# Two adjacency columns per transposed element, and eight-step cycles in the first pass of a graph attention kernel

## The chip, the cores and the metric

The kernel runs on one core of one Trainium2 chip. Times are device microseconds of one launch, from the first to the last instruction, as the hardware profiler takes them. A core has TensorE (PE in the profile; its weight loads are listed apart as PEld), VectorE (DVE), ScalarE (ACT), GpSimd (POOL) and SyncE (SP). POOL and SP are used here mostly to issue DMAs: POOL for those on the software queue, among them every DMA that changes the type of its data, SP for the others. Before the change the kernel took 2134.29 us, the median of 3 runs (2130.82 to 2136.55).

## What is computed

There are 4096 nodes with 512 features and a 0/1 adjacency of 4096 x 4096 in fp32, which is symmetric and has ones on its diagonal. Layer 0 is a graph attention layer with 8 heads of 64 features, layer 1 an attention within 32 graphs of 128 nodes. Each layer is followed by a residual sum and a normalisation. Layer 0, the part that matters here:

```python
feats = einsum('nf,hfo->hno', X, W)
dense = s_self[:, :, None] + s_neigh[:, None, :]     # per head, 4096 x 4096
dense = where(dense > 0, dense, 0.2 * dense)
attn = softmax(dense * A[None], axis=-1)
out = einsum('hij,hjo->hio', attn, feats) + b
```

The score of an edge is a sum of one number of node i and one of node j, so its exponential is a product, and the leaky slope makes it the larger of two products. The kernel uses this: per head and neighbour j it forms `q = max(p_i, d_j) * A[j, i]` and lets TensorE sum `q` against scaled features. No 4096 x 4096 exponential is ever taken.

## The kernel before, in words

The nodes are cut into 32 tiles of 128 neighbours j (a step works on one of them) and 4 chunks of 1024 nodes i. The order is fixed by hand on PE (its instructions keep the order of the program); the other engines' instructions are placed by a scheduler that moves them among each other.

**Setup** (to about 165 us). Eight blocks of four tiles. For block k, PE transposes the rows of x (`turn_rows`, L631), computes the features of four tiles (`features`, L699, four fp32 matmuls of 512 columns each), the two scores per head (`scores` L640 for the block after, and `exponentials` L654), and turns the exponentials of the self scores, p and u, from columns into rows (`rows_of_exponentials`, L689). ACT copies those rows to SBUF (`pu_row`, L693), from where a DMA writes them to DRAM. ACT and DVE make scaled features out of each tile (`scaled_features`, L706 to L730: `gst`, and `fst` on ACT L717 and DVE L718), and POOL writes them to DRAM as g_d and f_d. There are two buffers each for `fst` and `gst`, so the third `fst` of a block waits until the write of the first has landed. After blocks 4 and 5 POOL issues the first two adjacency loads (L758, L573).

**Four passes over the adjacency**, two heads each (`main_pass`). A pass runs over the 4 chunks, a chunk over its 32 steps in cycles of `wide` steps: 4 in passes 0 and 3, 8 in passes 1 and 2. In a cycle:

- DVE makes `q` for each step and each of the two heads (L1285); ACT makes a 0/1 `mark` of each (L1294), and DVE makes every eighth mark (L1290);
- PE sums the raw adjacency against the features into `accf` (L1305), then `q` against scaled features into `acc` (L1321), and every eight steps the marks into `dens` (L1335); in pass 0 also the row sums `ae` (L1346 to L1354, in the profile at L1348);
- the adjacency tiles `at` of the next cycle are brought, `wide - 2` of them after `accf` and the others at the cycle's end (`follow`, L1312 and L1355).

**Bringing a tile** (`bring`, L1051). In passes 1 to 3 it is a DMA from at_d. In pass 0 the adjacency comes from the input, where it has nodes i on rows, and is needed with j on partitions: POOL loads 1024 x 512 values and turns them into bf16 on the way (`a_bf`, L571 to L575, two buffers), PE transposes the eight 128 x 128 blocks of a step into PSUM (L1063), ACT casts them to fp32 (L1064), and POOL writes the tile to at_d for the later passes (L1065). `at` and `q` have six buffers each; passes 1 and 2 add six and two more (`ring`, `more`).

At the end of a chunk DVE takes the sums out of PSUM (`ys`), and small pieces of work (transposes L1128, L1147, L1170) are put among the matmuls of the next chunk. Layer 1 follows the last pass and is woven into its end.

Of the kernel before, what the change touches and what calls it, by code (L numbers as in the profile page):

```python
# [10 lines left out]
F32 = mybir.dt.float32  # L11
BF16 = mybir.dt.bfloat16
I32 = mybir.dt.int32
AF = mybir.ActivationFunctionType
# [5 lines left out]
P = 128  # L20
ALPHA = 0.2
# [374 lines left out]
F32R = mybir.dt.float32r  # L396
# [8 lines left out]
def adjacency_streamed_path(  # L405
# [29 lines left out]
    nc = tc.nc  # L435
    N, F = x.shape
    H, _, FH = W.shape
    NT = N // P
    FC = F // P
# [116 lines left out]
    def ring(name, pool, n):  # L556

        if name not in more:
            return pool
        k = turns[name] % (n + more[name][1])  # L560
        turns[name] += 1
        return pool if k < n else more[name][0]
# [1 line left out]
    ats = {}  # L564
    a_bs = {}
    pools = {}
    pools["adj"] = first_pass.enter_context(tc.tile_pool(name="adjp", bufs=2, side="right"))

    def load_adjacency(c, j):

        a_b = pools["adj"].tile([P, CT, 4 * P], BF16, name="a_bf")  # L571
        a_bs[c, j] = a_b
        return nc.gpsimd.dma_start(  # L573
            a_b, adj[ts(c, C), j * P : (j + 4) * P].rearrange("(t p) n -> p t n", p=P)
        )  # L575


    with tc.tile_pool(name="setup1", bufs=1, side="right") as one, tc.tile_pool(
# [2 lines left out]
        name="xtp", bufs=4, side="right"  # L581
    ) as xtp, tc.tile_pool(name="ps_setup", bufs=7, space=PSUM) as pss:
        NB = NT // 4
        xts, xTs, sts = {}, {}, {}

        def load_rows(k):
            xts[k] = []
# [62 lines left out]
        def exponentials(k):  # L650
            blk = slice(4 * k, 4 * k + 4)
            pts = pss.tile([P, 4, 2, H], F32, name="ps_set")
            for u in range(4):
                nc.tensor.matmul(  # L654
                    pts[:, u].rearrange("p k h -> p (k h)"),
                    sts[k][:, ts(u, P)],
                    stack,
                    start=(u == 0),
                    stop=True,
                    skip_group_check=True,  # L660
                )
            s_c, t_c = pts[:, :, 0, :], pts[:, :, 1, :]
            nc.scalar.activation(e_all[:, blk, 1, :], t_c, AF.Exp)
            nc.scalar.activation(e_all[:, blk, 0, :], t_c, AF.Exp, scale=ALPHA)
            nc.scalar.activation(d_all[:, blk, :], t_c, AF.Exp, scale=ALPHA - 1.0)
            nc.scalar.activation(u_all[:, blk, :], s_c, AF.Exp, scale=-ALPHA)
            nc.scalar.activation(p_all[:, blk, :], s_c, AF.Exp, scale=1.0 - ALPHA)


            nc.vector.tensor_scalar_mul(  # L670
                nb_all[:, blk, :], d_all[:, blk, :], -BIG * (1.0 + 2.0**-23)
            )
            eb = e_b[:, blk]
            for i in range(2):
                src = e_all[:, blk, i, :]
                rest = small.tile([P, 4, H], F32, name="rest")
                nc.vector.tensor_copy(eb[:, :, :, 3 * i], src)
                nc.vector.tensor_sub(rest, src, eb[:, :, :, 3 * i])
                nc.vector.tensor_copy(eb[:, :, :, 3 * i + 1], rest)
                nc.vector.tensor_sub(eb[:, :, :, 3 * i + 2], rest, eb[:, :, :, 3 * i + 1])  # L680
            nc.vector.tensor_copy(
                e_p[:, blk, :NE].rearrange("p j (m h) -> p j h m", h=H), eb[:, :, :, :3]
            )
            nc.vector.tensor_scalar_mul(eb[:, :, :, :3], eb[:, :, :, :3], -1.0)

        def rows_of_exponentials(k):
            pr = pss.tile([2 * H, 4, P], F32, name="ps_set")
            for u in range(4):
                nc.tensor.transpose(  # L689
                    pr[:, u, :], pu_all[:, 4 * k + u].rearrange("p k h -> p (k h)"), ident  # L690
                )
            row = one.tile([2 * H, 4 * P], F32, name="pu_row")
            nc.scalar.copy(row, pr.rearrange("p u n -> p (u n)"))  # L693
            nc.gpsimd.dma_start(pu_d[:, ts(k, 4 * P)], row)

        def features(k, u):
            pf = pss.tile([P, H * FH], F32, name="ps_set")
            for c in range(FC):
                nc.tensor.matmul(  # L699
                    pf, xTs[k][:, c, u, :], w_sb[:, c, :], start=(c == 0), stop=(c == FC - 1)  # L700
                )
            fb = three.tile([P, H, FH], F32, name="fb")
            nc.vector.tensor_add(fb.rearrange("p h o -> p (h o)"), pf, b_row)
            return fb
# [28 lines left out]
        for k in range(NB):  # L733
            if k + 1 < NB:
                load_rows(k + 1)
            fbs = [features(k, 0)]
            if k == 0:
                fbs.append(features(k, 1))
                scores(0)
            else:  # L740
                exponentials(k)
            if k + 1 < NB:
                turn_rows(k + 1)
            if k == 0:
                exponentials(0)
            scaled_features(k, 0, fbs[0])
            if k:
                fbs.append(features(k, 1))
            scaled_features(k, 1, fbs[1])
            fbs.append(features(k, 2))  # L750
            scaled_features(k, 2, fbs[2])
            if k + 1 < NB:
                scores(k + 1)
            rows_of_exponentials(k)
            fbs.append(features(k, 3))
            scaled_features(k, 3, fbs[3])
            if k in (4, 5):
                tc.keep_in_program_order(load_adjacency(0, 4 * (k - 4)))  # L758
        xsum = one.tile([P, FC], F32, name="xsum")
        nc.vector.tensor_reduce(xsum, xs, AX.X, OP.add)  # L760
# [289 lines left out]

    def bring(r, c, j):  # L1051

        at = ring("at", atp, 6).tile([P, C], F32R, name="at")
        ats[r, c, j] = at
        if r:
            nc.sync.dma_start(at.bitcast(F32), at_d[c, j])
            return
        if j % 4 == 0 and (c, j) not in a_bs:
            load_adjacency(c, j)
        a_b = a_bs[c, j - j % 4]  # L1060
        pt = misc([P, CT, P], BF16)
        for t in range(CT):
            nc.tensor.transpose(pt[:, t, :], a_b[:, t, ts(j % 4, P)], ident_b)  # L1063
        nc.scalar.copy(at, pt.rearrange("p t n -> p (t n)"))  # L1064
        nc.gpsimd.dma_start(at_d[c, j], at.bitcast(F32))  # L1065

    def load_block():

# [169 lines left out]
    def main_pass(r, ae=None, wide=4):  # L1238

        for c in range(NCH):  # L1240
# [19 lines left out]
            for j0 in range(0, NT, wide):  # L1260
# [41 lines left out]
                for j in cycle:  # L1302
                    for w in range(2):
                        for s in range(2):
# [4 lines left out]
                                start=(j == 0 and w == 0),  # L1309
                                stop=(j == NT - 1 and w == 1),  # L1310
                            )
                for x_ in follow[: wide - 2]:  # L1312
                    bring(*x_)
                if r:
                    pieces(c, j0 // 4, 0)
# [26 lines left out]
                if r == 0:  # L1342
                    for j in cycle:

                        a_j = ats[r, c, j].bitcast(BF16).rearrange("p (n k) -> p n k", k=2)
                        for s in range(2):  # L1346
# [5 lines left out]
                                start=(j < 2),  # L1352
                                stop=(j >= NT - 2),
                            )  # L1354
                for x_ in follow[wide - 2 :]:  # L1355
                    bring(*x_)
                first = (at_step - NT * NCH) // 4
                for group in range(first, first + wide // 4) if r else ():
                    if group == 0:
                        load_block()  # L1360
                        load_block()
                    for _ in range(1 + (group % 3 == 2)):
                        check_block(done[0])
                        done[0] += 1
                        load_block()
            ends.append(sums_to_rows(r, c, acc, accf, ae, u_row, 0.75 * wide))

    done = [0]
    with tc.tile_pool(name="ps_ae", bufs=1, space=PSUM) as psx, tc.tile_pool(
        name="aes", bufs=1  # L1370
    ) as pools["aes"]:
        ae = psx.tile([P, HB], F32, name="ae")
        nc.vector.memset(ae, 0.0)
        banks.append(psx)
        main_pass(0, ae)
        run_pieces(999.0)
        banks.remove(psx)
    first_pass.close()
    banks.extend([ctx.enter_context(tc.tile_pool(name="ps_misc2", bufs=2, space=PSUM))] * 2)
    with tc.tile_pool(name="keep_f", bufs=1) as keep:  # L1380
        with tc.tile_pool(name="more_at", bufs=MORE) as at2, tc.tile_pool(
            name="more_q", bufs=2
        ) as q2:
            more["at"], more["q"] = (at2, MORE), (q2, 2)
            for x_ in steps[NT * NCH : NT * NCH + 8]:
                bring(*x_)
            with tc.tile_pool(name="wl1", bufs=1, side="right") as wp:
                work.append(weights_of_layer_1(keep, wp))
                work.append(kind_of_graphs(wp))
                kind_of_scores(wp)  # L1390
                main_pass(1, wide=8)
                for gen in work:
                    for _ in gen:
                        pass
                work.clear()
            main_pass(2, wide=8)
            more.clear()
        with tc.tile_pool(name="lp", bufs=2) as lp, tc.tile_pool(
            name="lp1", bufs=1
        ) as lp1, tc.tile_pool(name="lp2", bufs=2) as lp2:  # L1400
            pools.update(lp=lp, lp1=lp1, lp2=lp2)
            main_pass(3)
            plan["K"] = kind_of_inputs(lp1)
            run_plan("bEpppaaRaaKKbbababaababbbb")


@with_exitstack
# [50 lines left out]
```

## Time and profile before

| | busy us | share of the span |
|---|---|---|
| PE | 2091.5 | 98% |
| DVE | 1660.8 | 78% |
| ACT | 1537.5 | 72% |
| POOL | 249.5 | 12% |
| span of the profiled run | 2136.1 | |
| adjacency loads on POOL (L573), 32 | 12.7 us to landing | |
| writes of `at` (L1065), 128 | 11.8 us to landing | |

A line of a group reads: line, engine, operation, what is written from what, shape, count, then busy us and mean ns of one, then the idle time of the engine just before and what ended it. A line of the timeline reads: start in us, length in us, engine, line, operation, names and shape, how often in a row; a bracket gives idle time before it and what ended it. A matmul's length in the profile contains its latency, and neighbours overlap; where it matters, the difference of starts is what PE spends. The lines of the DMA queues are packets, MB, and the time that the packets took as a share of 16 engines' span.

### The profile page before, as it was taken

To read this page: it belongs to the slowest core of one execution; us is meant where nothing else is said; L and a number is where in the kernel's file an instruction comes from. 1 tells how busy PE (TensorE), PEld (TensorE's weight loads), DVE (VectorE), ACT (ScalarE), POOL (GpSimd) and SP (SyncE) were. 2 spreads that over 40 slices of the span, in tenths; PEclk is the share of its full clock that TensorE was granted. 3 is DMA by queue.
4 is the path that set the end of the run, shared out by engine and by line. 5 is a ranking of instruction groups with operands and counts; after the bars stand their busy time and mean duration, and the time that the engine had idled before them with its cause. 6 is when DMAs were issued, how large, how long until landed. Compare 5 with 4: busy or idle time off the path is not lost. (4 is left out here: it accounts for less than half of the span.)

```text
span 2136.1 us, 39020 instructions
## 1 busy us (share of the span) xinstructions
PE 2091.5 (98%) x15492; PEld 1036.8 (49%) x15492; DVE 1660.8 (78%) x2024; ACT 1537.5 (72%) x1820; POOL 249.5 (12%) x391
## 2 busy tenths in 40 slices
PE   8999999999999999999999999999999999999987
PEld 4545455555555444544454454444444444445443
DVE  5557777778688878799999999999974884886554
ACT  3337777878777988789998989999876566567420
POOL 2332222222210000000000000000310210110110
PEclk9999999999999999999999999999999999999999
DMA  8889999999999998789999999989964774674211
GB/s 249 277 236 293 321 294 287 300 272 307 270 296 320 337 320 273 259 291 348 332 325 334 312 338 332 331 290 357 320 227 150 239 246 144 218 270 163 70 47 42
DMA packets 207885, 568.13 MB, mean 266 GB/s; under 512 B 25292, under 2 KB 66252, under 8 KB 207692
## 3 DMA queue, kind: packets, MB, share of 16 engines
q1 hardware_dynamic: 140748, 425.79, 58.0%
q0 software_dynamic: 62784, 138.69, 23.5%
q8 instruction: 124, 2.03, 0.4%
q10 hardware_dynamic: 4160, 1.05, 0.2%
q14 instruction: 69, 0.57, 0.1%
HBM read 491.79 MB, written 107.22 MB: 280 GB/s over the span
## 5 line engine op out<-in xcount | busy, mean ns | idle before, releaser
L1285 DVE SCALAR_TENSOR_TENSOR q<-p_row,d_all,at 128x1024 f32<-128x1024 f32 x1024 | 1244.6, 1279 | 213.2 <-PE acc L1321 138.7
L1294 ACT ACTIVATE mark<-q,nb_all 128x1024 fp8e4<-128x1024 f32 x896 | 995.3, 1143 | 242.4 <-DVE q L1285 220.6
L1321 PE MATMUL acc<-q,g_s 128*32 128x512 f32 x8192 | 906.7, 593 | 3.0 <-DVE q L1285 2.5
L1321 PEld LDWEIGHTS acc<-q,g_s 128*32 128x32 f32 x8192 | 260.6, 110 | 591.5 <-issue 528.4
L1305 PE MATMUL accf<-at,f_s 128*128 128x512 f32 x2048 | 499.2, 398 | 2.0 <-DMA f_s<-f_d 1.7
L1305 PEld LDWEIGHTS accf<-at,f_s 128*128 128x128 f32 x2048 | 377.1, 189 | 113.2 <-issue 29.3
L1079 ACT ACTIVATE ck<-ck,neg_half_f 128x1024 f32<-128x1024 f32 x128 | 145.9, 1140 | 21.9 <-DMA ck<-in_adj_dram 21.7
L1080 ACT ACTIVATE ck<-ck,neg_quarter 128x1024 f32<-128x1024 f32 x128 | 146.3, 1143 | 1.8
L1064 ACT CAST at<-ps_m 128x1024 fp32r<-128x1024 bf16 x128 | 122.7, 1010 | 6.3 <-PE ps_m L1063 4.5
L1335 PE MATMUL dens<-mark,e_b 128*6 128x512 fp8e4 x2048 | 125.1, 381 | 0.0
L1006 PE MATMUL ps_m<-wvT,x1T 128*128 128x512 f32 x256 | 114.3, 594 | 4.1 <-DVE parts L1150 4.0
L934 PE MATMUL ps_m<-x1T,M_sb 128*128 128x512 f32 x256 | 115.9, 607 | 1.8 <-ACT x1T L915 1.8
L699 PE MATMUL ps_set<-w_sb_f,xT_f 128*128 128x512 f32 x256 | 114.5, 600 | 0.0
L1183 POOL DMA_DIRECT2D hs_d<-hst x12 | 10.7, 895 | 838.3 <-DVE hst L1171 736.1
L1290 DVE TENSOR_SCALAR mark<-q,d_all 128x1024 fp8e4<-128x1024 f32 x128 | 95.8, 748 | 3.2
L1335 PEld LDWEIGHTS <-e_b 128*6 128x6 bf16 x2048 | 53.4, 86 | 83.1 <-issue 40.1
L1065 POOL DMA_DIRECT2D at_d<-at x128 | 68.6, 536 | 172.9 <-ACT at L1064 171.0
L717 ACT ACTIVATE fst<-fb 128x512 fp32r<-128x512 f32 x32 | 20.3, 634 | 93.6 <-DMA f_d<-fst 65.6
L934 PEld LDWEIGHTS ps_m<-x1T,M_sb 128*128 128x128 f32 x256 | 49.0, 194 | 65.4 <-issue 62.5
L1006 PEld LDWEIGHTS ps_m<-wvT,x1T 128*128 128x128 f32 x256 | 47.7, 190 | 60.1 <-issue 57.4
L699 PEld LDWEIGHTS ps_set<-w_sb_f,xT_f 128*128 128x128 f32 x256 | 48.3, 194 | 54.2 <-issue 53.8
L1014 DVE TENSOR_TENSOR v_t<-ps_m,bv_row 128x512 f32<-128x512 f32 x32 | 21.8, 681 | 63.5 <-PE ps_m L1006 63.5
(169 smaller groups left out, 1204.9 us busy)
## 6 DMA issues: line engine op xcount, KB each, us to landing
at<-at_d SPq DMA_DIRECT2D x384, 512.0 KB, 5.8
ck<-in_adj_dram SPq DMA_DIRECT2D x128, 512.0 KB, 5.4
f_s<-f_d SPq DMA_DIRECT2D x128, 512.0 KB, 7.7
at_d<-at POOLq DMA_DIRECT2D x128, 512.0 KB, 11.8
g_s<-g_d SPq DMA_DIRECT2D x128, 256.0 KB, 5.8
a_bf<-in_adj_dram POOLq DMA_DIRECT2D x32, 1024.0 KB, 12.7
f_d<-fst POOLq DMA_DIRECT2D x32, 512.0 KB, 6.4
p_row<-pu_d SPq DMA_DIRECT2D x32, 512.0 KB, 6.9
```

Source lines behind the costliest of these rows:

```text
L699: nc.tensor.matmul(pf, xTs[k][:, c, u, :], w_sb[:, c, :], start=(c == 0), stop=(c == FC - 1))
L934: nc.tensor.matmul(pz, L1["M"][:, f, ts(c, P)], x1T[:, f, :], start=(f == 0), stop=(f == FC - 1),)
L1006: nc.tensor.matmul(pv, x1T[:, f, ts(u, P)], L1["wvT"][:, f, :], start=(f == 0), stop=(f == FC - 1),)
L1064: nc.scalar.copy(at, pt.rearrange("p t n -> p (t n)"))
L1079: tc.keep_in_program_order(nc.scalar.activation(ck, ck, AF.Square, bias=neg_half))
L1080: nc.scalar.activation(ck, ck, AF.Abs, bias=neg_quarter, accum_out=binp[:, k : k + 1])
L1285: nc.vector.scalar_tensor_tensor(q, p_row[h], d_j, ats[r, c, j].bitcast(F32), op0=OP.max, op1=OP.mult)
L1290: nc.vector.tensor_scalar(mark, q, d_j, None, op0=OP.is_gt, saturate=False)
L1294: nc.scalar.activation(mark, q, AF.Sigmoid, bias=nb_all[:, j, hh : hh + 1], scale=BIG, saturate=False,)
L1305: nc.tensor.matmul(accf[:, s, :], f_s[j // 4][:, j % 4, w, :], ats[r, c, j][:, ts(s, HB)], start=(j == 0 and w == 0), stop=(j == NT - 1 an ...
L1321: nc.tensor.matmul(acc[o : o + 32, s, :], g_s[j // 4][:, j % 4, h, o % FH : o % FH + 32], qs[j, h][:, ts(s, HB)], start=(j == 0), stop=(j ...
L1335: nc.tensor.matmul(dens[lo : lo + 6, :], e_b[:, j, 2 * r + h, :], marks[j, h][:, ts(s, HB)], start=(j == 0), stop=(j == NT - 1),)
```

## The change

The adjacency holds only zeros and ones, which an 8-bit float holds exactly. The load in pass 0 now makes 8-bit floats, and two neighbouring columns of a row are taken together as one 16-bit element. A transpose moves 16-bit elements unchanged, so one transpose now turns 256 columns instead of 128, and the number of transposes halves. What lands on a partition is a pair: an even and an odd node. ACT casts the even bytes into one `at` tile and the odd bytes into another. So a tile of neighbours is no longer 128 nodes in a row, but the even or the odd ones among 256.

Everything that belongs to a neighbour has to follow that order: features and exponentials are computed for the even and odd nodes by weights with a step of two (`tile_j`). What belongs to a node i keeps the plain order: the row copy puts p and u back into it, and a new function, `columns_of_exponentials`, turns these rows into columns again for the chunk ends.

The loads get a third buffer and a third early issue after block 6. Pass 0 now has cycles of eight steps like passes 1 and 2, with their rings of 12 and 8 buffers; four tiles are brought after `accf` and four at the cycle's end. The pools of those rings are opened before pass 0. The aim is to take transposes and the switches between short cycles off PE in the first pass.

```diff
-    pools["adj"] = first_pass.enter_context(tc.tile_pool(name="adjp", bufs=2, side="right"))
+    pools["adj"] = first_pass.enter_context(tc.tile_pool(name="adjp", bufs=3, side="right"))
...
 
-        a_b = pools["adj"].tile([P, CT, 4 * P], BF16, name="a_bf")
+        a_b = pools["adj"].tile([P, CT, 4 * P], FP8, name="a_b8")
...
-        xts, xTs, sts = {}, {}, {}
+        xts, xTs, sts, pu_js, rows = {}, {}, {}, {}, {}
+
+        def tile_j(x, u):
+
+            return x.rearrange("p (q n k) -> p q n k", q=2, k=2)[:, u // 2, :, u % 2]
...
-                    sts[k][:, ts(u, P)],
+                    tile_j(sts[k], u),
...
-            nc.scalar.activation(u_all[:, blk, :], s_c, AF.Exp, scale=-ALPHA)
-            nc.scalar.activation(p_all[:, blk, :], s_c, AF.Exp, scale=1.0 - ALPHA)
+            pu_j = pu_js[k] = two.tile([P, 4, 2, H], F32, name="pu_j")
+            nc.scalar.activation(pu_j[:, :, 1, :], s_c, AF.Exp, scale=-ALPHA)
+            nc.scalar.activation(pu_j[:, :, 0, :], s_c, AF.Exp, scale=1.0 - ALPHA)
...
-            row = one.tile([2 * H, 4 * P], F32, name="pu_row")
-            nc.scalar.copy(row, pr.rearrange("p u n -> p (u n)"))
+                    pr[:, u, :], pu_js[k][:, u].rearrange("p k h -> p (k h)"), ident
+                )
+            row = rows[k] = one.tile([2 * H, 4 * P], F32, name="pu_row")
+            nc.scalar.copy(
+                row.rearrange("p (q n k) -> p q k n", q=2, k=2),
+                pr.rearrange("p (q k) n -> p q k n", q=2),
+            )
             nc.gpsimd.dma_start(pu_d[:, ts(k, 4 * P)], row)
+
+        def columns_of_exponentials(k):
+            pc = pss.tile([P, 4, 2 * H], F32, name="ps_set")
+            for u in range(4):
+                nc.tensor.transpose(pc[:, u, :], rows[k][:, ts(u, P)], ident[: 2 * H, : 2 * H])
+            nc.vector.tensor_copy(
+                pu_all[:, 4 * k : 4 * k + 4].rearrange("p u k h -> p u (k h)"), pc
+            )
 
...
                 nc.tensor.matmul(
-                    pf, xTs[k][:, c, u, :], w_sb[:, c, :], start=(c == 0), stop=(c == FC - 1)
+                    pf,
+                    tile_j(xTs[k][:, c].rearrange("p u n -> p (u n)"), u),
+                    w_sb[:, c, :],
+                    start=(c == 0),
+                    stop=(c == FC - 1),
                 )
...
             rows_of_exponentials(k)
             fbs.append(features(k, 3))
             scaled_features(k, 3, fbs[3])
-            if k in (4, 5):
+            columns_of_exponentials(k)
+            if k in (4, 5, 6):
                 tc.keep_in_program_order(load_adjacency(0, 4 * (k - 4)))
...
     def bring(r, c, j):
 
-        at = ring("at", atp, 6).tile([P, C], F32R, name="at")
-        ats[r, c, j] = at
         if r:
+            at = ats[r, c, j] = ring("at", atp, 6).tile([P, C], F32R, name="at")
             nc.sync.dma_start(at.bitcast(F32), at_d[c, j])
+            return
+        if j % 2:
             return
         if j % 4 == 0 and (c, j) not in a_bs:
             load_adjacency(c, j)
-        a_b = a_bs[c, j - j % 4]
+        pairs = a_bs[c, j - j % 4].rearrange("p t n -> p (t n)").bitcast(BF16)
+        pairs = pairs.rearrange("p (t k n) -> p t k n", t=CT, k=2)[:, :, j % 4 // 2, :]
         pt = misc([P, CT, P], BF16)
         for t in range(CT):
-            nc.tensor.transpose(pt[:, t, :], a_b[:, t, ts(j % 4, P)], ident_b)
-        nc.scalar.copy(at, pt.rearrange("p t n -> p (t n)"))
-        nc.gpsimd.dma_start(at_d[c, j], at.bitcast(F32))
+            nc.tensor.transpose(pt[:, t, :], pairs[:, t, :], ident_b)
+        both = pt.rearrange("p t n -> p (t n)").bitcast(FP8).rearrange("p (n k) -> p n k", k=2)
+        for k in range(2):
+            at = ats[r, c, j + k] = ring("at", atp, 6).tile([P, C], F32R, name="at")
+            nc.scalar.copy(at, both[:, :, k])
+            nc.gpsimd.dma_start(at_d[c, j + k], at.bitcast(F32))
...
-                for x_ in follow[: wide - 2]:
+                first = wide // 2 if r == 0 or wide == 4 else 6
+                for x_ in follow[:first]:
                     bring(*x_)
...
-                for x_ in follow[wide - 2 :]:
+                for x_ in follow[first:]:
                     bring(*x_)
...
     done = [0]
+    keep = ctx.enter_context(tc.tile_pool(name="keep_f", bufs=1))
+    wide_passes = ExitStack()
+    at2 = wide_passes.enter_context(tc.tile_pool(name="more_at", bufs=MORE))
+    q2 = wide_passes.enter_context(tc.tile_pool(name="more_q", bufs=2))
+    more["at"], more["q"] = (at2, MORE), (q2, 2)
...
-        main_pass(0, ae)
+        main_pass(0, ae, wide=8)
...
-    with tc.tile_pool(name="keep_f", bufs=1) as keep:
-        with tc.tile_pool(name="more_at", bufs=MORE) as at2, tc.tile_pool(
-            name="more_q", bufs=2
-        ) as q2:
-            more["at"], more["q"] = (at2, MORE), (q2, 2)
-            for x_ in steps[NT * NCH : NT * NCH + 8]:
-                bring(*x_)
...
+    more.clear()
+    wide_passes.close()
```

## The prediction

> **What bounds the kernel now.** I read the page first: what is busy, and who waits.
>
> ```profile
> PE 2091.5 (98%) x15492; PEld 1036.8 (49%) x15492; DVE 1660.8 (78%) x2024; ACT 1537.5 (72%) x1820; POOL 249.5 (12%) x391
> ```
>
> TensorE (PE) is busy 98% of the span and its groups show almost no idle time, so a stage ends when its matmuls end, and what a change takes off PE's stream is worth its full length while the feeders keep up. Second, the groups kept apart by shape, for what the change halves:
>
> ```profile
> L1064 ACT CAST at<-ps_m 128x1024 fp32r<-128x1024 bf16 x128 | 122.7, 1010 | 6.3 <-PE ps_m L1063 4.5 <-issue 1.1 <-ACT mark L1294 0.7
> L1063 PE MATMUL ps_m<-ident_b,a_bf 128*128 128x128 bf16 x1024 | 69.0, 221 | 1.3 <-ACT at L1064 1.3
> ```
>
> 1024 transposes cost 69 us of PE, all in the first pass (165 to 632 us). Third, PE's timeline over eight steps of that pass, for the spacing of the starts:
>
> ```profile
> 384.34 0.63 PE L1348 MATMUL ae<-at,e_p 128*25 128x512 bf16 x8
> 384.90 1.07 PE L1063 MATMUL ps_m<-ident_b,a_bf 128*128 128x128 bf16 x16
> 385.78 3.92 PE L1305 MATMUL accf<-at,f_s 128*128 128x512 f32 x16
> 389.54 1.07 PE L1063 MATMUL ps_m<-ident_b,a_bf 128*128 128x128 bf16 x16
> 390.54 7.07 PE L1321 MATMUL acc<-q,g_s 128*32 128x512 f32 x64
> 397.43 1.91 PE L1335 MATMUL dens<-mark,e_b 128*6 128x512 fp8e4 x32
> 399.15 0.63 PE L1348 MATMUL ae<-at,e_p 128*25 128x512 bf16 x8
> 399.72 1.07 PE L1063 MATMUL ps_m<-ident_b,a_bf 128*128 128x128 bf16 x16
> 400.59 3.96 PE L1305 MATMUL accf<-at,f_s 128*128 128x512 f32 x16
> 404.40 1.07 PE L1063 MATMUL ps_m<-ident_b,a_bf 128*128 128x128 bf16 x16
> ```
>
> No bracket with a wait: the matmuls follow one another. Fourth, the DMA queues between 200 and 600 us, because this is the pass that both loads and writes the adjacency:
>
> ```profile
> q0 software_dynamic: 44954, 87.43, 83.8%
> q1 hardware_dynamic: 10135, 29.40, 21.2%
> ```
>
> Last, the setup, where the change adds a wait. ScalarE (ACT) and PE around block 5:
>
> ```profile
> 118.64 0.63 ACT L717 ACTIVATE fst<-fb 128x512 fp32r<-128x512 f32 x1 [2.58 <-DVE fb L703]
> 129.89 0.63 ACT L717 ACTIVATE fst<-fb 128x512 fp32r<-128x512 f32 x1 [10.62 <-DMA f_d<-fst]
> 130.43 0.57 ACT L648 COPY st<-ps_set 128x512 f32<-128x512 f32 x1
> 130.89 0.57 ACT L693 COPY pu_row<-ps_set 16x512 f32<-16x512 f32 x1
> ```
>
> ```profile
> 122.19 0.60 PE L689 MATMUL ps_set<-ident_f,pu_all 128*16 128x128 f32 x4
> 122.63 7.03 PE L699 MATMUL ps_set<-w_sb_f,xT_f 128*128 128x512 f32 x16
> 131.04 1.06 PE L654 MATMUL ps_set<-stack,st 128*128 128x16 f32 x8 [1.38 <-ACT st L648]
> ```
>
> The row copy `pu_row` queues behind an `fst` that waits 10.6 us for a DMA; today nothing on PE waits for that copy.
>
> [...] here 16 transposes take 1.07 us, 67 ns each, and I use that. [...]
>
> **The change, part by part.**
>
> *Half the transposes.* 512 go, at 67 ns: 34.2 us of nominal PE time; what is visible is less, since bursts overlap at their ends. So I add up starts instead.
>
> *Cycles of eight.* Before, from the starts above and their neighbours: accf to transposes 3.76, to acc 1.00, acc to the next 6.89; twice, that is 23.30; dens 1.72, ae twice 0.57, transposes to accf twice 0.87: 27.90. Measured over 15 cycles of eight, 183.13 to 618.66 us less 13.5 us for the pieces of work of the chunk ends: 28.14; the 0.24 are casts that came late. After, the third pass, which has cycles of eight already, gives accf 7.55 (1043.13 to 1050.68) and acc 13.76. So 7.52 + 1.00 + 13.76 + 1.72 + 1.14 + 0.87 = 26.0 us. Saved: 2.1 x 16 = 34 us.
>
> *Can the feeders hold 26.0?* The built program's order on ACT per cycle is five marks, four casts (second half of this cycle), two marks, four casts (first half of the next), seven marks. ACT: 14 marks at 1.06 (five take 5.31) and 8 casts at 0.96 make 22.5 us. VectorE (DVE): 16 q at 1.21 and two marks at 0.75, 20.9 us. Both fit. The tight place: with acc starting at 0, DVE ends this cycle's q at 12.4, five more by 18.5, their marks end at 19.6; the casts end at 20.6, 21.5, 22.5, 23.4 and accf wants them at 21.3, 22.2, 23.1, 24.1. Spare 0.6 us. At the three chunk ends DVE first spends 2.5 us on `ys`, so there I expect a miss: 2 us in all. A cast that reads every other byte touches the same PSUM bytes as today's, so I leave it at 0.96; the far end is double.
>
> *8-bit loads.* The same 2 KB are read per row piece, half as much is written; three buffers instead of two start a load about 1.5 cycles ahead of its use, against 12.7 us to landing. I cost the load at nothing: it lies beside the matmuls. Per eight steps the DMAs move 10.35 MB (adjacency read 4.19, transposed write 4.19, f and g 1.57, rows 0.39): 367 GB/s at 28.2 us, 398 at 26.0. The software queue, 83.8% busy, would come to 91%.
>
> *Rings and pools.* Twelve `at` and eight `q` buffers, which passes 1 and 2 use already: nothing.
>
> *Setup, strided weights.* 256 weight loads of L699 take 190 ns beside a matmul spacing of 430; even doubled they stay hidden. Nothing, up to double.
>
> *Setup, transposes back to columns.* 32 more, 0.13 us each (as the eight of L1170 in 1.04): 0.5 us per block, 4 us. The DVE copy lies in DVE's idle time.
>
> *Setup, the new wait.* PE now does the column transposes right after the fourth tile's features, 3.5 us after the row transposes, and waits for the row copy. Behind it stand the next block's features (3.5 us), its exponentials and everything else on PE. Comparing the end of the copy with the end of those features in each block of the trace: in time in blocks 0, 1, 3, 7; late by 1.2 in block 2 and 1.5 in block 4; in blocks 5 and 6, where an adjacency load sits ahead of the f_d writes in the queue, by 5.3 and 5.0. In block 5 PE already lost 1.38, so the net is 131.5 + 0.5 + 3.5 - 131.0 = 4.5. In block 6 PE then comes later while the DMA does not: I take 1.5 of a possible 4.5. A wait of 1.8 us for x rows at 73 us absorbs block 2. Sum 1.2 + 1.5 + 4.5 + 1.5 - 1.8 + 4 = 11 us; 4 if the copies are in time, 20 if all come in full. The third early load delays block 7's `fst`, but PE is late by then too.
>
> *Start of the pass.* Eight casts instead of four stand before the first full cycle: +1 us.
>
> Sum: -34 + 2 + 11 + 1 = -20, so 2114 us.
>
> **Rivals.** *The DMA becomes the bound.* Shares of 83.8 and 21.2 add up to more than one, and 398 GB/s over a whole pass would equal the best stretch now. For it: landing of the transposed writes is 11.8 us against 3.5 at best. Against: the two queues overlap, no matmul waits for an adjacency load (0.3 us in all), and the written bytes shrink. If the pass keeps 28.2 us per cycle, only the setup loss is left: 2134 + 12 = 2146, slower; half way, 2130. *The setup wait costs little*, because the lighter loads let the f_d writes land sooner: -34 + 2 + 4 + 1, 2107. *ACT becomes the bound*: casts at 1.9 us make 15.2 + 14.8 = 30 us per cycle, 1.9 more than before: 2134 + 30 + 12 = 2176. Same bytes read speak against it. *Casts just late every cycle*, by 1 us: 2130.
>
> **How the numbers follow.** Forecast 0.55. Cheap setup 0.15. DMA fully 0.07, half way 0.08. Late casts 0.08. ACT 0.07. Below 2128 (faster by over 0.3%): forecast, cheap setup, a small part of the half-way cases: 0.74. Between 2128 and 2141: most of the two middle cases, 0.12. Slower: 0.14. The range takes in setup from 4 to 20 us and the middle cases: 2101 to 2133.
>
> **What would show it.** 512 transposes at the same 67 ns; starts of accf 26.0 us apart in the first pass, without waits in brackets; casts at about 1 us; adjacency landing near 12 us. In the setup, PE idle before the column transposes with the row copy as releaser, longest in blocks 5 and 6, and the first accf about 12 us later than 169.4. Passes 1 to 3 unchanged. Wrong, if accf waits for casts or for loads in most cycles, if the casts exceed 1.2 us, or if L699's spacing leaves 430 ns.

## The result, and the profile after

The changed kernel takes 2122.8 us (median of 6 runs, 2117.65 to 2125.04), the kernel before in the same comparison 2135.56 us (6 runs, 2130.82 to 2140.69): a ratio of 0.9937, with a 95% interval of 0.9918 to 0.9956. That is 9 to 18 us less, 12.8 by the medians. The profiled executions differ by 17.2 us (spans 2136.1 and 2118.9); what follows takes those 17 us apart.

The page of the kernel after, busy times:

```profile
PE 2065.7 (97%) x15012; PEld 1023.2 (48%) x15012; DVE 1659.5 (78%) x2032; ACT 1538.1 (73%) x1820; POOL 249.1 (12%) x391
```

PE lost 26 us of work and is still busy 97% of the span. The groups of the kernel after, kept apart by shape:

```profile
L1090 ACT CAST at<-ps_m 128x1024 fp32r<-128x1024 fp8e4 x128 | 120.1, 1025 | 14.9 <-issue 11.0 <-DMA f_d<-fst 2.2 <-PE ps_m L1086 0.9
L1086 PE MATMUL ps_m<-ident_b,a_b 128*128 128x128 bf16 x512 | 36.1, 224 | 4.2 <-DVE hst L1197 2.4 <-ACT at L1090 1.4 <-DVE S_col L792 0.5
```

Half the transposes (512, each of 128 x 128 pairs as 16-bit elements) at the same 67 ns (16 in the 1.07 us below), and a cast that reads every other byte of PSUM takes 1025 ns where the bf16 cast took 1010, each in the mean. One cycle of eight steps on PE's timeline after:

```profile
234.45 7.58 PE L1331 MATMUL accf<-at,f_s 128*128 128x512 f32 x32
241.87 1.07 PE L1086 MATMUL ps_m<-ident_b,a_b 128*128 128x128 bf16 x16
242.87 13.94 PE L1348 MATMUL acc<-q,g_s 128*32 128x512 f32 x128
256.63 1.91 PE L1362 MATMUL dens<-mark,e_b 128*6 128x512 fp8e4 x32
258.36 1.08 PE L1375 MATMUL ae<-at,e_p 128*25 128x512 bf16 x16
259.37 1.07 PE L1086 MATMUL ps_m<-ident_b,a_b 128*128 128x128 bf16 x16
260.25 2.10 PE L1331 MATMUL accf<-at,f_s 128*128 128x512 f32 x8
```

From 234.45 to 260.25 are 25.80 us with no bracket, so no wait; 11 of the 16 spacings in the pass lie between 25.78 and 25.85 (the others are the first, the last and the three chunk ends). The DMA queues after, between 200 and 600 us (packets, MB, share):

```profile
q0 software_dynamic: 46989, 79.09, 85.1%
q1 hardware_dynamic: 10272, 29.36, 20.2%
```

The software queue is hardly fuller than before (83.8%), though the cycles are shorter. The MB are those that a DMA writes: the 8-bit loads read as much as the bf16 loads and write half (512 KB each in the profile for 1024), and the sum fell from 87.4 to 79.1 MB. Per eight steps, chunk ends included, the queue was busy 83.8% of 29.3 us before, or 24.6 us, and 85.1% of 27.5 us after, or 23.4 us. Last the setup, PE and then ACT, at the end of block 2 after:

```profile
67.36 3.61 PE L715 MATMUL ps_set<-w_sb_f,xT_f 128*128 128x512 f32 x8
74.78 0.61 PE L707 MATMUL ps_set<-ident_f,pu_row 16*128 16x16 f32 x4 [3.81 <-ACT pu_row L698]
75.32 6.65 PE L715 MATMUL ps_set<-w_sb_f,xT_f 128*128 128x512 f32 x8
```

```profile
73.13 0.63 ACT L737 ACTIVATE fst<-fb 128x512 fp32r<-128x512 f32 x1 [9.13 <-DMA f_d<-fst]
73.67 0.57 ACT L652 COPY st<-ps_set 128x512 f32<-128x512 f32 x1
74.13 0.60 ACT L698 COPY pu_row<-ps_set 16x512 f32<-16x512 f32 x1
```

This is the new wait: ACT stands 9.13 us before an `fst` whose buffer is still being written out, the row copy stands behind it, and now PE stands behind the row copy for 3.81 us. The eight features that follow take 6.65 us instead of 3.61. The stretches of that time in the trace after show another clock (length, then busy times of PE, PEld, DVE, ACT and POOL, then PE's granted clock, DMA share and GB/s):

```profile
67.00:71.00 4.00, 3.97 (x12) 1.69 (x12) 0.69 (x1) 0.00 (x0) 0.41 (x1) 1.00 1.02 350
76.00:77.00 1.00, 1.00 (x2) 0.34 (x1) 0.25 (x1) 0.23 (x1) 0.51 (x2) 0.50 0.99 295
```

PE's clock was granted in full (1.00) before the wait and at half (0.50) after it, until about 81 us.

A chunk end of the kernel after, on PE:

```profile
334.12 1.95 PE L1154 MATMUL ps_m<-comb,aes 128*128 128x9 f32 x16
335.93 0.64 PE L1173 MATMUL ps_m<-ident_f,dcs 128*128 128x128 f32 x4
337.34 1.94 PE L1196 MATMUL ps_m<-ident_f,ys 128*128 128x128 f32 x8 [0.78 <-DVE rd L1186]
339.21 2.61 PE L1362 MATMUL dens<-mark,e_b 128*6 128x512 fp8e4 x32
...
342.96 1.21 PE L1086 MATMUL ps_m<-ident_b,a_b 128*128 128x128 bf16 x16 [0.22 <-DVE hst L1197]
```

All four pieces of the last chunk come in one cycle. PE waits for DVE within them (0.78), and the transposes wait for `hst`, the DVE multiplication that frees the small PSUM tiles of the `ys` transposes. At this end `dens` also runs partly at half clock (2.61 us instead of 1.91; the stretch from 338 to 340 us has 0.50), but the clock does not set the length: at the third chunk end `dens` takes 1.90 us, the transposes wait 1.81 us for `hst` instead of 0.22, and the end costs 6.4 us all the same. Before, the second chunk end:

```profile
428.71 1.06 PE L1170 MATMUL ps_m<-ident_f,ys 128*128 128x128 f32 x8 [0.78 <-DVE rd L1160]
429.70 1.90 PE L1335 MATMUL dens<-mark,e_b 128*6 128x512 fp8e4 x32
431.43 0.62 PE L1348 MATMUL ae<-at,e_p 128*25 128x512 bf16 x8
431.98 1.07 PE L1063 MATMUL ps_m<-ident_b,a_bf 128*128 128x128 bf16 x16
```

The wait of 0.78 was there, the wait for `hst` was not. The second and third end cost 3.7 us each, the first, with `dens` at half clock (2.80 us; 0.50 granted from 312 to 314 us), 5.3. DVE from the step that ends the wait of 0.78 to `hst`, first before (second end), then after (first end):

```profile
428.56 1.28 DVE L1285 SCALAR_TENSOR_TENSOR q<-p_row,d_all,at 128x1024 f32<-128x1024 f32 x1
429.76 0.17 DVE L1161 TENSOR_TENSOR rd<-parts,rd 128x16 f32<-128x16 f32 x1
429.96 0.18 DVE L1162 TENSOR_TENSOR rd<-rd,z_all 128x16 f32<-128x16 f32 x1
430.17 0.25 DVE L1163 RECIPROCAL rd<-rd 128x16 f32<-128x16 f32 x1
430.51 1.29 DVE L1171 TENSOR_TENSOR hst<-ps_m,rd 128x512 f32<-128x512 f32 x2
```

```profile
337.20 1.28 DVE L1311 SCALAR_TENSOR_TENSOR q<-p_row,d_all,at 128x1024 f32<-128x1024 f32 x1
338.39 0.17 DVE L1187 TENSOR_TENSOR rd<-parts,rd 128x16 f32<-128x16 f32 x1
338.48 1.28 DVE L1311 SCALAR_TENSOR_TENSOR q<-p_row,d_all,at 128x1024 f32<-128x1024 f32 x1
339.68 0.17 DVE L1188 TENSOR_TENSOR rd<-rd,z_all 128x16 f32<-128x16 f32 x1
339.76 1.28 DVE L1311 SCALAR_TENSOR_TENSOR q<-p_row,d_all,at 128x1024 f32<-128x1024 f32 x1
340.96 0.25 DVE L1189 RECIPROCAL rd<-rd 128x16 f32<-128x16 f32 x1
341.12 1.19 DVE L1311 SCALAR_TENSOR_TENSOR q<-p_row,d_all,at 128x1024 f32<-128x1024 f32 x1
342.23 1.28 DVE L1197 TENSOR_TENSOR hst<-ps_m,rd 128x512 f32<-128x512 f32 x2
```

Four `q` stand among the small steps that `hst` needs, where there was one. From the `ys` transposes to the next ones PE takes 5.62 us at all three ends after, and 3.27 us before (4.91 at the first).

The 17.2 us, by the starts of `accf` in both traces:

| term | forecast, us | profiled pair, us | how measured |
|---|---|---|---|
| 16 cycles of eight steps | -34 | -38.4 | 28.19 (a cycle of 13.39 and one of 14.80) to 25.79 each |
| three chunk ends | +2 | +6.5 | beyond the cycle: 4.2 each before, 6.4 after |
| start of the pass | +1 | +2.8 | 1.7 between last setup feature and first accf, 1.1 in the first cycle |
| end of the pass | 0 | +2.2 | 33.51 - 28.19 before, 33.33 - 25.79 after |
| setup, to the last feature | +11 | +10.2 | 162.0 to 172.2 us |
| passes 1 to 3 and layer 1 | 0 | -0.6 | 1497.3 to 1496.75 us |

### The profile page after: what moved, and what is told of

Same layout as the page of the kernel before. It is cut to its first block, busy times and chain, and to the rows that moved or that the text cites. A ratio compares the mean times of both kernels' runs of the same rounds, so it can differ in the third digit from the quotient of the medians.

```text
span 2118.9 us, 38159 instructions
## 1 busy us (share of the span) xinstructions
PE 2065.7 (97%) x15012; PEld 1023.2 (48%) x15012; DVE 1659.5 (78%) x2032; ACT 1538.1 (73%) x1820; POOL 249.1 (12%) x391
## 5 line engine op out<-in xcount | busy, mean ns | idle before, releaser
L1348 PEld LDWEIGHTS acc<-q,g_s 128*32 128x32 f32 x8192 | 265.0, 110 | 596.1 <-issue 535.7
L1331 PE MATMUL accf<-at,f_s 128*128 128x512 f32 x2048 | 492.9, 397 | 1.0 <-DMA f_s<-f_d 0.8
L1090 ACT CAST at<-ps_m 128x1024 fp32r<-128x1024 fp8e4 x128 | 120.1, 1025 | 14.9 <-issue 11.0
L715 PE MATMUL ps_set<-w_sb_f,xT_f 128*128 128x512 f32 x256 | 118.9, 613 | 0.0
## 6 DMA issues: line engine op xcount, KB each, us to landing
at_d<-at POOLq DMA_DIRECT2D x128, 512.0 KB, 14.7
a_b<-in_adj_dram POOLq DMA_DIRECT2D x32, 512.0 KB, 17.1
```

What stands on the lines that cost most here:

```text
L715: nc.tensor.matmul(pf, tile_j(xTs[k][:, c].rearrange("p u n -> p (u n)"), u), w_sb[:, c, :], start=(c == 0), stop=(c == FC - 1),)
L1090: nc.scalar.copy(at, both[:, :, k])
L1331: nc.tensor.matmul(accf[:, s, :], f_s[j // 4][:, j % 4, w, :], ats[r, c, j][:, ts(s, HB)], start=(j == 0 and w == 0), stop=(j == NT - 1 an ...
L1348: nc.tensor.matmul(acc[o : o + 32, s, :], g_s[j // 4][:, j % 4, h, o % FH : o % FH + 32], qs[j, h][:, ts(s, HB)], start=(j == 0), stop=(j ...
```

## Experiments

All were run against the kernel before; ratios are to it, with 95% intervals. In each the first accf, the cycle and the end of the pass are from its own profiled execution.

**1. The halved transposes with cycles of four.**

```diff
-        main_pass(0, ae, wide=8)
+        main_pass(0, ae)
```

> The change with cycles of four in the first pass (the longer rings stay). Theory, from the terms of the prediction: the halved transposes carry the gain, the length of the cycle carries none. Eight steps then cost 2 x (3.76 + 0.50 + 6.89 + 0.57 + 0.44) + 1.72 = 26.0 us, as with cycles of eight (25.8 in the trace after); the chunk ends get 2 us each and the start 1.5 us back: 2112 to 2120 us, faster than the changed kernel by 3 to 10 us. Rival: cycles of eight carry about half of the gain, since short cycles leave casts late: 27 us or more per eight steps, 2135 us or more.

Measured: 2125.14 us, 0.9955 (0.9942 to 0.9967), as good as the whole change within the intervals, so the eight-step cycles show no gain of their own in the total. Eight steps take 26.15 us (12.20 and 13.95), so the transposes carry 2.04 of the 2.40 us and the long cycle 0.36. The range was missed by 5 us on the high side. Chunk ends cost 5 to 7 us, not the 4.2 of before; the part of the expectation that gave 2 us back there failed. The wait for `hst` is gone here: no `q` stands among DVE's small steps at the ends.

**2. Cycles of eight with the old transposes.** The kernel before, the pools of the rings opened early as in the change, and:

```diff
-        main_pass(0, ae)
+        main_pass(0, ae, wide=8)
...
-                for x_ in follow[: wide - 2]:
+                first = wide // 2 if r == 0 or wide == 4 else 6
+                for x_ in follow[:first]:
```

> The kernel before with nothing but cycles of eight in the first pass (bf16 adjacency, 1024 transposes, four tiles after accf and four at the end of the cycle, rings of 12 and 8). Theory: eight steps cost 7.52 + 2.1 + 13.76 + 1.72 + 1.14 + 1.95 = 28.2 us, no gain over 28.2; chunk ends, start and end of the pass cost up to 9 us more: 2134 to 2145 us. Rival: cycles of eight carry about half of the gain: 27 us per eight steps, 2125 us or less.

Measured: 2237.76 us, 1.048 (1.0466 to 1.0494). Both expectations fell: eight steps take 34.0 us, 6 us more than before. PE at the end of a cycle in this kernel, then ACT:

```profile
282.41 1.07 PE L1063 MATMUL ps_m<-ident_b,a_bf 128*128 128x128 bf16 x16
286.43 0.61 PE L1063 MATMUL ps_m<-ident_b,a_bf 128*128 128x128 bf16 x8 [2.95 <-ACT at L1064]
287.34 1.01 PE L1063 MATMUL ps_m<-ident_b,a_bf 128*128 128x128 bf16 x8 [0.31 <-ACT at L1064]
```

```profile
280.68 4.80 ACT L1294 ACTIVATE mark<-q,nb_all 128x1024 fp8e4<-128x1024 f32 x4 [0.71 <-DVE q L1285]
285.38 2.82 ACT L1064 CAST at<-ps_m 128x1024 fp32r<-128x1024 bf16 x3
```

Four tiles are brought at once. Two go into PSUM, the third waits for a buffer, which the first cast frees, and that cast stands behind four marks. In the first pass the small PSUM tiles (`misc`) have two buffers. The old transposes need one per tile, the paired ones one per two tiles: with pairs, four tiles fit. The waits for casts make 4.3 us per cycle here (2.95, 0.31, 0.70, 0.31), and the accf after them takes 8.8 us instead of 7.6; the mean granted clock is 0.95 from 254 to 288 us and 0.94 from 390 to 500. My new theory was that this, not the long cycle, costs the 6 us.

**5. The same, two tiles at a time** (told here since it answers the second).

```diff
+                    if r == 0 and j == j0 + 3:
+                        for x_ in follow[:2]:
+                            bring(*x_)
...
-                for x_ in follow[:first]:
+                for x_ in follow[2 if r == 0 else 0 : first]:
...
+                    if r == 0 and j == j0 + 3:
+                        for x_ in follow[4:6]:
+                            bring(*x_)
...
-                for x_ in follow[first:]:
+                for x_ in follow[6 if r == 0 else first :]:
```

The first addition stands in the loop of accf, the second in that of acc; the matmuls of `ae` move ahead of acc.

> The kernel before with cycles of eight as in the second experiment, but its tiles brought two at a time: amid accf, after accf (with ae moved there), amid acc and at the end of the cycle. Theory: cycles of eight with one tile per transpose lose 6 us per cycle because four tiles at a time need four PSUM buffers and there are two, so that PE waits in mid-burst for a cast that stands behind marks on ACT. Two at a time fit: about 28.2 us per cycle again, 2130 to 2150 us. Rival: eight marks and casts per cycle with the longer rings upset ACT's order whatever the bursts are: 33 us or more per cycle, above 2215 us.

Measured: 2158.75 us, 1.0101 (1.0086 to 1.0117). The cycle is 28.1 us again, as the theory of the two buffers has it, while the total lies above its range and far below the rival's: the first cycle alone takes 43.0 us, 12.9 of them a wait for an adjacency load, and a chunk end costs 7.25 us. So a long cycle brings the old transposes nothing in any form tried.

**3. The columns one block later.**

```diff
-            columns_of_exponentials(k)
+            if k:
+                columns_of_exponentials(k - 1)
...
-            row = rows[k] = one.tile([2 * H, 4 * P], F32, name="pu_row")
+            row = rows[k] = two.tile([2 * H, 4 * P], F32, name="pu_row")
```

and the last block's columns after the loop.

> The change with the column transposes of a block done one block later, when its row copy has long been made (two buffers for the row). Theory: the waits of PE for the row copy go (0.8 + 3.8 + 0.7 + 2.9 + 0.9 = 9.1 us in the trace after), and with them 2.9 us that the features of block 2 took longer just after the longest wait; some 4 us come back as waits for the f_d writes. First accf near 173 instead of 181.3 us, 2112 to 2118 us. Rival: the setup is tied to the f_d writes and the row copy wait only took the place of that wait: first accf stays at 179 to 182 us, 2121 to 2124 us.

Measured: 2115.45 us, 0.9901 (0.9885 to 0.9917), in the range. No column transpose waits any more; features and columns end at 162.2 us, against 162.0 before the change. Some 1.7 us of that are luck: near 75 us the kernel before fell to half clock (0.50 from 76 to 78 us, 13 transposes of x in 3.04 us) and this execution did not (1.00 from 76 to 80 us, 1.64). So of the 10 us that the setup lost, about 8 were the wait and what came of it, and the 32 column transposes (3.2 us of PE) cost about 2. The first accf came at 176.0 and not 173: after the setup PE waits 3.85 us for `S_col` on DVE, behind a `gst` that waited 5.5 us for a g_d write.

**4. The pieces apart.**

```diff
-                    run_pieces(0.75 * wide)
+                    run_pieces(0.75 * wide if r else 1.6)
...
-            ends.append(sums_to_rows(r, c, acc, accf, ae, u_row, 0.75 * wide))
+            ends.append(sums_to_rows(r, c, acc, accf, ae, u_row, 0.75 * wide if r else 1.6))
```

> The change with the small pieces of a chunk end spread over two cycles of the first pass (two in each) instead of all in one. Theory: a chunk end costs 6.35 us beyond its cycle now and 4.2 before, because the pieces wait for each other through VectorE and hold their PSUM buffers; apart they cost their own 4.3 us on PE: 3 x 2 us less, 2115 to 2119 us. Rival: the 2 us are the late casts and q of the first cycle of a chunk, whatever the pieces do: 2121 to 2124 us.

Measured: 2107.0 us, 0.9866 (0.985 to 0.9882), more than expected. The same chunk end in this kernel, two pieces now and two a cycle later:

```profile
333.11 1.95 PE L1154 MATMUL ps_m<-comb,aes 128*128 128x9 f32 x16
334.92 0.64 PE L1173 MATMUL ps_m<-ident_f,dcs 128*128 128x128 f32 x4
335.49 1.90 PE L1362 MATMUL dens<-mark,e_b 128*6 128x512 fp8e4 x32
...
361.38 1.09 PE L1196 MATMUL ps_m<-ident_f,ys 128*128 128x128 f32 x8
```

No wait is left, `dens` takes the 1.90 us of full clock and a chunk end costs 3.6 us instead of 6.4, some 8 us for three. What cost the time was four pieces in one place: apart, the transposes no longer wait for `hst`. The profiled executions differ by 13 us: 8.2 at the chunk ends, 1.0 by the second cycle's start, 4.4 in passes 1 to 3, -0.5 at the end of the pass. The medians differ by 16. Why passes 1 to 3 were shorter the traces don't show; the same passes took 1494 to 1499 us in the other executions here and 1492.4 in this one. That part stays open.

**6 and 9. More adjacency loads.** Beside each load a second, unused one of half the columns:

```diff
+        if "again" in pools:
+            again = pools["again"].tile([P, CT, 2 * P], FP8, name="again")
+            nc.gpsimd.dma_start(
+                again, adj[ts(c, C), j * P : (j + 2) * P].rearrange("(t p) n -> p t n", p=P)
+            )
```

> The change with a second, unused adjacency load of half the columns beside each load of the first pass (16 x 2 x 2.1 MB more read, some 20% more of the bytes that the DMAs move in the pass). Theory: PE still sets the cycle and the DMAs have room: landings grow (17 us to about 25), cycles stay at 25.8, 2120 to 2128 us. Rival, that the DMA is at its limit: the cycle grows by half of the added traffic or more, 28 us, 2155 us or more.

Measured: 2204.14 us, 1.0309 (1.029 to 1.0328), but it tells nothing of the DMAs' limit: the scheduler put most of the unused loads ahead of the needed ones on POOL, where they waited for each other 107 us in all; PE stood 32 and 29 us for an adjacency load. Between 430 and 620 us, when the unused loads had run out, the cycles were 25.8 again. In the ninth the unused load is held behind the needed one (`keep_in_program_order`).

> The sixth experiment mended: there the unused loads were moved ahead of the needed ones on POOL and blocked them; here each keeps its place behind the needed load beside which it is issued. Theory: the DMAs have room for 20% more bytes in the first pass: the cycle stays at 25.8 us, landings grow from 17 us to some 20, 2120 to 2130 us. Rival, that the DMA is at its limit: accf or the transposes wait for adjacency loads in most cycles, 27 us or more per cycle, above 2140 us.

Measured: 2162.06 us, 1.0115 (1.0099 to 1.013). My expectation missed. The first cycles (28.6 us, then three of 25.8) use up what was loaded ahead, then about every second one takes 35 to 36 us. The software queue between 208 and 500 us, and the first such wait on PE:

```profile
q0 software_dynamic: 50809, 54.88, 100.0%
```

```profile
299.12 1.89 PE L1094 MATMUL ps_m<-ident_b,a_b 128*128 128x128 bf16 x16 [7.13 <-DMA a_b<-in_adj_dram]
```

A full queue gives 31.3 us per eight steps here, chunk ends included ((628.56 - 284.42) / 11); the changed kernel has 27.5 us at 85.1%, or 23.4 us of queue. So, as an estimate from these shares, the added loads took 7.9 us or a third more of the queue's time: they are a quarter more bytes if loads count as read (2.1 on 8.4 MB), a tenth if they count as written (0.5 on 5.2), in row pieces half as long. The changed kernel had 4.1 us of the queue to spare in each cycle, 15%. The DMAs were not its bound. POOL itself stood another 17 us of the 292 us for unused loads, so not all of the waits need come from the full queue.

**7. The third early load later as well**, issued after the setup instead of after block 6, on top of the third:

```diff
-            if k in (4, 5, 6):
+            if k in (4, 5):
...
+    tc.keep_in_program_order(load_adjacency(0, 8))
```

> The columns one block later as in the third experiment, and the third early adjacency load issued after the setup instead of after block 6. Theory: that load stands ahead of block 7's g_d and f_d writes in the queue and makes DVE wait 5.5 us for g_d, which ends in the 3.85 us that PE waits for S_col; without it the first accf comes at about 172.5 us (176.0 in the third experiment), 2110 to 2114 us. Rival: the writes of block 7 are late anyway: first accf at 175 to 176 us, 2114 to 2117 us.

Measured: 2117.22 us, 0.99 (0.9884 to 0.9917), above the theory's range and just above the rival's, with the first accf at 176.5 us, yet the wait for `S_col` is gone, as the theory said. The time went elsewhere: at 75 to 78 us PE waits for rows of x (1.95 us in three pieces), and the next 13 transposes take 3.04 us instead of 1.64, as in the kernel before at half clock, and 16 features 8.54 instead of 7.04. The third experiment had waited 1.57 us at this place and kept its clock (1.00). What sets the clock there was not tried (the last section says what the traces show of it), so the value of the edit stays open.

**8, 10, 11. Together.** The eighth is the seventh with the pieces apart; the tenth adds buffers for the rows of x; the eleventh holds ACT's first marks of the second pass behind the copy of the row sums.

```diff
-        name="xtp", bufs=4, side="right"
+        name="xtp", bufs=6, side="right"
...
+                            if (r, c, j0) == (1, 0, 0):
+                                tc.keep_in_program_order(made)
```

> The seventh experiment with the pieces spread over two cycles as in the fourth. Theory: the gains add up, 8 us per pass at the chunk ends and some 9 us at the start: 2098 to 2104 us. Rival: the earlier start is taken back by casts and the f_d writes in the first cycle: 2105 to 2109 us, no better than the fourth experiment.

> The eighth experiment with six buffers for the rows of x in the setup instead of four. Theory: PE waits 1.9 us for x rows at 77 us and then runs the next 13 transposes and 16 features at a lower clock (3.0 and 8.5 us instead of 1.6 and 7.0); with the rows in time both go, some 4 us: first accf near 172 us, 2097 to 2101 us. Rival: the rows come late because of the DMAs, not for want of buffers, or the time is lost at the next wait of the setup: 2102 to 2106 us.

> The tenth experiment with ACT's first marks of the second pass held behind the copy of the row sums aes at the end of the first. Theory: PE waits 3.4 us for aes there because one mark, which itself waits for q, stands ahead of the copy; without it some 2 us at the end of the first pass: 2095 to 2099 us. Rival: the marks then come late for the first cycle of the second pass and the time is lost again: no better than the tenth experiment.

Measured: 2103.93 us, 0.9836 (0.9818 to 0.9854); 2100.93 us, 0.9828 (0.9814 to 0.9841); 2097.96 us, 0.9815 (0.9802 to 0.9828). Each is in its range, though the intervals of neighbours overlap. The eighth got there without the gain that was expected at the start: it still met the half clock (0.50 from 77 to 82 us, 8.54 us for the 16 features at 80 us); the tenth has no wait for rows of x and starts accf at 170.7 instead of 176.0 us. In the eleventh PE's wait for `aes` falls from 3.4 to 0.7 us and the last stretch of the pass from 34.1 to 30.5 us. The first cycle of the second pass is no longer for it (24.4 us in both), so the time is not lost again there. It is the best version here, some 26 us better than the change by the two ratios.

## Why the prediction was right

The direction, the mechanism and the range held; the forecast of 2114 was 9 us low. That the sum came so close is in part luck: of its -20 us the profiled pair shows -17, the cycles gave 4.4 us more than forecast, and the chunk ends, the start and the end of the pass together took 8.5 us more. By its own steps:

- *Half the transposes, cycles of eight*: forecast 26.0 us from PE's own starts, measured 25.79. Two of its terms came out smaller, where one long burst took the place of two short ones: accf 7.42 us for 7.52, `ae` 1.01 for 1.14. The base was 28.19, not 28.14, so the gain is 38.4 and not 34 us. The first experiment shows that the transposes give nearly all of it, as the sum said (27.90 before became 26.0 only by the transposes). What the sum did not say: the two edits are not independent. The second experiment would have been costed at no loss by the same sum and lost 102 us, because it adds up what PE does and not how many PSUM buffers a burst needs.
- *Feeders*: right. Four casts in a row take 3.76 us, 0.94 each against 0.96 taken, and no bracket stands in the cycle. That a cast costs the same because it touches the same PSUM bytes was an estimate; the times show that the two casts are alike, not why.
- *8-bit loads, costed at nothing*: right in time, wrong in detail. Loads landed in 17.1 us (12.7 before) instead of near 12, and the transposed writes in 14.7 (11.8 before); no cycle waits for a load. What the third buffer has to do with that was not tried. The software queue rose to 85.1% and not 91%, since it was busy 23.4 us per eight steps and not 24.6; the ninth experiment shows what happens when it is full. The 398 GB/s set beside the best stretch mixed two counts: the forecast counted the loads as they are read, the profile counts what they write (117 MB in the 400 us before, 294 GB/s). And the best stretch of the trace before is higher: from 384 to 387.5 us it has 408, from 308 to 310 us 418.
- *Strided weights, nothing*: right. 16 features take 7.04 us at full clock, 7.03 before; a weight load has 203 ns in the mean, 194 before (medians 197 and 190).
- *Setup wait*: 11 forecast, 10.2 in this execution, but by luck in the parts. Blocks 5 and 6 were to lose most, 4.5 and 1.5, and waited 2.9 and 0.9; block 2, which a later wait for x rows was to absorb, waited 3.8 and then lost another 2.9 at half clock (0.50). The first and fourth experiments have the same setup and end it at 167.7 and 168.1 us, 6 us later than before, so that term was nearer to 6 than to 11 there. The third shows that the wait is the cause.
- *Third early load*: "PE is late by then too" held only as long as the columns made PE late; in the third experiment it comes out as 3.85 us.
- *Chunk ends*: the term of the sum that was mis-sized, 6.5 us against 2. I counted late casts there, and no wait for a cast shows at a chunk end after. The fourth experiment shows that the pieces are the cause: all four run in one place in the cycle and wait for each other through DVE. Why this costs more than before is read from the traces: every kernel here that has eight-step cycles and the pieces in one place takes 5.62 us from the `ys` transposes to the next ones, with old transposes (second and fifth) as with new, while the kernel before and the first experiment, with cycles of four, take 3.3 us at two ends of three and 4.9 at the other, which in the kernel before is the one at half clock. That the four `q` ahead of `hst` are the reason was not tried by itself.
- *End of the pass*: not in the sum at all, 2.2 us. One mark of the next pass, itself waiting for q, stands ahead of the copy of the row sums on ACT; the eleventh experiment takes the wait away.
- *Start of the pass*: forecast 1 us, measured 2.8; the eight casts and the setup's last pieces were not taken apart further.

Of the rivals, the DMA as the bound was not far off: 15% of the software queue was left. Casts at 1.9 us and casts late in every cycle are refuted by the trace after. The setup rival, cheap because f_d writes land sooner, had part of it: ACT's longest wait for an f_d write in block 5 fell from 10.6 to 8.2 us, while in block 2 it rose from 6.5 to 9.1.

## What to carry to other kernels

Adding up starts on the bounding engine forecast the steady cycle to a per cent here, but such a sum holds only while each burst finds its buffers (the second experiment's cycle took 34.0 us for a sum of 28.2): count PSUM tiles per burst before lengthening a cycle. What was lost here was lost at the seams (setup, chunk ends, pass ends), where a short copy stood behind a long wait on its engine; moving its consumer one stage later took the wait away, for one more buffer. To learn how near a hidden transfer is to being the bound, add to it in its place in the queue, and see which cycle is the first to wait.

## What was not expected of the hardware

A wait of PE cost more than its length: after the 3.81 us in block 2 the granted clock was 0.50 for 6.83 us, and eight features took 6.65 us instead of 3.61. In the traces before and after, every recorded stretch of half clock that ends within the span lasts 3.41 us (seven of them), 6.83 us (six) or 10.24 us (one in each). Block 2 after, cut at the changes of the clock and every 3.41 us (length, PE busy, granted clock, DMA share, GB/s):

```profile
71.05:74.46 3.41, 0.00 (x0) 1.00 1.06 257
74.46:77.87 3.41, 3.09 (x7) 0.50 1.04 329
77.88:81.29 3.41, 3.41 (x5) 0.50 0.98 372
81.29:84.70 3.41, 3.41 (x27) 1.00 0.21 83
```

The length of a wait does not tell by itself what the clock does after it. Waits of 2.93 us (after, block 5) and 2.77 us (fourth, block 2) left it at 1.00. After 1.87 us (eighth) it was 0.50, and after 1.95 us in three pieces (seventh) the transposes took the 3.04 us that they take at half clock. At the chunk ends, with 0.78 us among short pieces, it was 0.50 at two of three ends after and at one of three before. What decides it is not shown. The same setup ran slow in different places: in block 2 in the kernel after (eight features in 6.65 us instead of 3.7) and in block 5 in the first and fourth experiment (5.40, after waits of 3.35 and 2.98 us). Eight features alone took 1.7 to 3 us longer there.

On the software queue a quarter more bytes as read (a tenth as written), in row pieces half as long, took by the estimate above a third more of the time: for these loads, which change the type, the bytes alone did not tell what the queue paid. Whether the shorter pieces or the change of type is the reason was not tried.
